# A mixture-of-experts bias that travels with the expert's weights, and a residual that is stored before the routing

## The chip, the cores and the metric

The kernel runs on one core of a Trainium2 chip, and its time is the device time of one execution in microseconds (us). The core has five engines that each work off their own list of instructions in order: TensorE (PE; its weight loads are shown as PEld), VectorE (DVE), ScalarE (ACT), GpSimd (POOL) and SyncE (SP, which here only issues transfers). Transfers between the device's memory and the on-chip memory (SBUF) are done by 16 DMA engines. Results of TensorE land in a second on-chip memory, PSUM, and are fetched from there by DVE or ACT.

## The reference, cut to what matters

Two layers work on 2 x 56 x 56 tokens of 256 numbers. Layer 0 is a neighbourhood attention. Layer 1 has a gated linear attention with a residual, and then the part that the change is in, a mixture of eight experts of which each token uses two:

```python
logits = xf @ gate_w + gate_b
probs = softmax(logits)
top2_vals, top2_idx = top_k(probs, 2)
cw = zeros((N, 8)).at[rows, top2_idx].add(top2_vals)
for w1, b1, w2, b2, we in experts:            # we = cw's column of this expert
    acc += we[:, None] * (gelu(xf @ w1 + b1) @ w2 + b2)
out = x + acc                                 # the layer adds its residual x
```

The second bias b2 (256 numbers for each expert) therefore comes to a token as `cw[token] @ b2`, or, which is the same sum, as `we * b2` beside each of its two experts' results.

## The kernel before, in words

Layer 0 takes about the first 480 us and isn't touched. Layer 1 (`layer_1(False)`, the usual branch) goes over the tokens in 14 steps of 448 (`NST`, `BLK`; four tiles of 112 tokens). For each step, `before_pairs(s)` loads x (`x_acc`, line 730), normalizes it and projects it to q, k and v; `attention(s)` computes the attention, adds its output to x (line 982) and calls `route(s, x)`. `route` normalizes x into `xs`, computes the gate, ranks the eight experts of every token and works out, for both experts that a token uses, the row in which it stands in that expert's region of a buffer `xs_d` in device memory. Eight indirect transfers on POOL's queue (line 1246) write the normalized tokens there. `listed(s)` then lists which tiles of 256 rows (`SL`) have become full. After that `route` adds the second biases: it transposes the combine weights `cw` (line 1260), copies them to SBUF on ACT (line 1262), multiplies them with all eight biases on TensorE (line 1265, `p_b` in the profile), adds the product to x on DVE (line 1266), and stores x to `out` in two transfers on POOL's queue (line 1269).

The experts' tiles are worked off by the generator `experts()`, 56 tiles in all. `fetch(k)` loads a tile's tokens `xg` (line 1372) and the weights `wj` of its expert (line 1376) on SP's queue, two tiles ahead. `gather` transposes the tokens (lines 1386 and 1390), `hidden` computes the first matrix product and the gelu (lines 1400 and 1407), and `results` the second product (line 1431). Before that product `results` makes the tile's row numbers (`rows_e`, line 1415) and combine weights (`own_e` and `cws`, line 1419) on DVE. Each half tile `ye` of 128 rows is scaled out of PSUM by DVE (line 1439), and an indirect transfer on POOL's queue adds it to its rows of `out` (line 1440).

The function `together` interleaves these generators: while attention(s) runs, it advances before_pairs(s+1) and the expert tiles that earlier steps have filled (none in steps 0 to 2, then three or four a step). Two more tiles follow the last step, then the padding of the last rows, and 18 more tiles. This gives a priority to each instruction; the order that stands on each engine is fixed when the kernel is built, and is not always that of the code. Semaphores keep whatever depends on each other in order. Two transfers that both write `out` (or `xs_d`) count as dependent, so each waits for the one before it to have landed.

Buffers: the pool p3 has three buffers (`x_acc`, `xs`, `xg`, `wj`), p6 has six (`ye`, `rows_e`), p2 has two (`cws`), and six PSUM buffers (`mm`) are shared by all the products of a step and a tile.

Of the kernel before, what the change touches and what calls it, by code (L numbers as in the profile page):

```python
# [14 lines left out]
F32 = mybir.dt.float32  # L15
I32 = mybir.dt.int32
U32 = mybir.dt.uint32
AF = mybir.ActivationFunctionType
ALU = mybir.AluOpType
# [4 lines left out]
P = 128  # L24
NB = 2
IMG = 56
L = IMG * IMG
C = 256
NG = 2
# [11 lines left out]
TT = 112  # L41
# [7 lines left out]
NF = FF // P  # L49
# [105 lines left out]
def hybrid_kernel(ctx: ExitStack, tc: tile.TileContext, t: dict, out: bass.AP):  # L155
# [11 lines left out]
    def load(pool, name, shape, src, eng=None, dt=F32):  # L167
        dst = pool.tile(shape, dt, name=name)
        (eng or nc.sync).dma_start(out=dst, in_=src)
        return dst  # L170
# [32 lines left out]
    wgb = load(const, "wgb", [NB * NH, 1], t["L1_attn_wg_b"].unsqueeze(0).to_broadcast([NB * NH, 1]))  # L203
    gw = load(const, "gw", [P, NG, NE], t["L1_ffn_gate_w"].rearrange("(k p) e -> p k e", p=P))
    gb = load(const, "gb", [TT, NE], t["L1_ffn_gate_b"].unsqueeze(0).to_broadcast([TT, NE]))
    b2 = load(const, "b2", [NE, C], t["L1_ffn_b2"])
    before = load(const, "before", [TT, TT], t["before"])
    cand = load(const, "cand", [P, 8 * NE + NX + NE], t["cand"])
    c_row, c_exp, c_num, c_num1 = (
# [429 lines left out]
    def layer_1(general):  # L639
        with (  # L640
# [503 lines left out]

            def route(s, x):


                nonlocal n_prev, c_prev, at_prev
                xs = p3.tile([TT, NTI, ROW], F32, tag="xs", name="xs")
                nc.gpsimd.memset(xs[:, :, CWC + NE :], 0.0)  # L1150
                xT = yield from norm_T(x, "xT_f", p1, xs)
# [103 lines left out]
                listed(s)  # L1255
                yield

                pc = ps_m.tile([NE, NTI, TT], F32, tag="mm", name="p_cw")
                for i in range(NTI):
                    nc.tensor.transpose(pc[:, i, :], cw[:, i, :], ident[:TT, :TT])  # L1260
                cwT = p1.tile([NE, NTI, TT], F32, tag="cwT", name="cwT")
                nc.scalar.copy(cwT, pc)
                for i in range(NTI):
                    ps = ps_m.tile([TT, C], F32, tag="mm", name="p_b2")
                    nc.tensor.matmul(ps, lhsT=cwT[:, i, :], rhs=b2, start=True, stop=True)
                    nc.vector.tensor_tensor(x[:, i, :], ps, x[:, i, :], ALU.add)
                    yield
                for b in range(NB):
                    nc.gpsimd.dma_start(
                        out=out[b * L + s * BT : b * L + (s + 1) * BT].rearrange(  # L1270
                            "(i p) e -> p i e", p=TT
                        ),
                        in_=x[:, b * 2 : (b + 1) * 2, :],
                    )

            def listed(s):


# [74 lines left out]
            def fetch(j):  # L1353

                ent, k = listed_at.pop(j)
                known = "the lists hold rows of the regions and experts alone"
                row = nc.values_load(
                    ent[0:1, 0, k : k + 1],
                    engines=[mybir.EngineType.SP],
                    min_val=0,  # L1360
                    max_val=NE * RG,
                    skip_runtime_bounds_check_because=known,
                )
                exp = nc.values_load(
                    ent[0:1, 1, k : k + 1],
                    engines=[mybir.EngineType.SP],
                    min_val=0,
                    max_val=NE - 1,
                    skip_runtime_bounds_check_because=known,
                )  # L1370
                xg = p3.tile([P, SL // P, ROW], F32, tag="xg", name="xg")
                nc.sync.dma_start(
                    out=xg, in_=xs_d[bass.ds(row, SL), :].rearrange("(u p) c -> p u c", p=P)
                )
                wj = p3.tile([P, NG * FF + NF * C + NF], F32, tag="wj", name="wj")
                nc.sync.dma_start(
                    out=wj, in_=t["we"][bass.ds(exp, 1)].rearrange("o p c -> (o p) c")
                )
                return xg, wj
# [12 lines left out]

            def hidden(xT, wj):
                w1 = wj[:, : NG * FF].rearrange("p (k f) -> p k f", k=NG)
                b1 = wj[:, NG * FF + NF * C :]
                hT = p2.tile([P, NF, SL], F32, tag="hT", name="hT")
                for f in range(NF):
                    ph = ps_h.tile([P, SL], F32, tag="mm", name="p_h")
                    for k in range(NG):
                        nc.tensor.matmul(  # L1400
                            ph,
                            lhsT=w1[:, k, f * P : (f + 1) * P],
                            rhs=xT[:, k, :],
                            start=k == 0,
                            stop=k == NG - 1,
                        )
                    nc.scalar.activation(hT[:, f, :], ph, AF.Gelu, bias=b1[:, f : f + 1])  # L1407
                    yield
                return hT

            def results(j, hT, xg, wj):
                w2 = wj[:, NG * FF : NG * FF + NF * C].rearrange("p (k o) -> p k o", k=NF)

                rows = p6.tile([P, SL // P], I32, tag="rows_e", name="rows_e")
                nc.vector.tensor_copy(rows, xg[:, :, TOK : TOK + 1].rearrange("p u o -> p (u o)"))  # L1415
                cws = p2.tile([P, SL // P], F32, tag="cws", name="cws")
                own = p2.tile([P, NE], F32, tag="own_e", name="own_e")
                for u in range(SL // P):
                    nc.vector.scalar_tensor_tensor(
                        own,  # L1420
                        c_e,
                        l_exp[:, j : j + 1],
                        xg[:, u, CWC : CWC + NE],
                        ALU.is_equal,
                        ALU.mult,
                        accum_out=cws[:, u : u + 1],
                    )
                for u in range(SL // P):
                    py = ps_h.tile([P, C], F32, tag="mm", name="p_y")
                    for f in range(NF):  # L1430
                        nc.tensor.matmul(  # L1431
                            py,
                            lhsT=hT[:, f, u * P : (u + 1) * P],
                            rhs=w2[:, f, :],
                            start=f == 0,
                            stop=f == NF - 1,
                        )
                    y = p6.tile([P, C], F32, tag="ye", name="ye")
                    nc.vector.tensor_scalar_mul(y, py, cws[:, u : u + 1])  # L1439
                    nc.gpsimd.indirect_dma_start(  # L1440
                        out=out[:, :],
                        out_offset=bass.IndirectOffsetOnAxis(
                            ap=rows[:, u : u + 1].bitcast(U32), axis=0
                        ),
                        in_=y,
                        in_offset=None,
                        compute_op=ALU.add,
                    )
                    yield
# [142 lines left out]
```

## Time and profile before

The time is 1860.25 us, the median of three runs (1853.78 to 1864.68). The profiled execution spans 1865.8 us.

| engine | busy us | share of the span |
|---|---|---|
| PE (matmul) | 1504.1 | 81% |
| PEld (weight load) | 1075.6 | 58% |
| DVE | 936.4 | 50% |
| ACT | 626.3 | 34% |
| POOL | 448.5 | 24% |

| stretch of the span, us | what runs there |
|---|---|
| 0 to 480 | layer 0 |
| 480 to 700 | steps 0 to 2 of layer 1, without expert tiles |
| 700 to 1625 | steps 3 to 13, with 36 expert tiles |
| 1625 to 1866 | the last 20 tiles |

How to read it: a line of a group gives the line of the code, the engine, the operation, the tensor written and the tensors read, the number of instructions, their summed busy time, the mean duration of one, the idle time of the engine just before them, and what ended most of that idle time. A line of the timeline gives start, duration, engine and line, and in brackets the idle time before it. In a list of waits, "A <- B: 10.0, 3, 5.0" says that A waited for B three times, 10.0 us in total and 5.0 us at most. A busy share is a mean over stages with different limits, so a stage is read by the wait that ends last in it.

### The profile page before, as it was taken

What the parts mean: (1) busy time and instruction counts of PE and PEld (TensorE: products, weight loads), DVE (VectorE), ACT (ScalarE), POOL (GpSimd) and SP (SyncE); (2) the same over time, 40 slices, a digit from 0 to 9 for tenths busy, and PEclk for the clock granted to TensorE, in tenths of its full rate; (3) what the DMA queues carried; (4) which work ended last, traced back from release to release, by engine and by line L of the source; (5) the groups of instructions that cost most, each with busy time, mean ns of one, the idle gap of its engine ahead of it and who ended that gap; (6) DMA issues with size and microseconds to landing.
All of it is one profiled execution on the core that took longest, in us unless ns stands there. A gap on an engine that the chain in (4) does not pass through costs nothing. (4 is left out here: it accounts for less than half of the span.)

```text
span 1865.8 us, 28574 instructions
## 1 busy us (share of the span) xinstructions
PE 1504.1 (81%) x10840; PEld 1075.6 (58%) x10840; DVE 936.4 (50%) x2787; ACT 626.3 (34%) x1125; POOL 448.5 (24%) x496
## 2 busy tenths in 40 slices
PE   0899999999487778898798879888887888778781
PEld 0466776789254445565465556556565656666670
DVE  3455566654466775655637373746465464411110
ACT  0233433432333233443325333433344241322220
POOL 2123333332101101213131322213131313322232
PEclk9989999975688779899899989898899899989885
DMA  7345554452101103234242414232333324276542
GB/s 227 119 147 168 161 152 145 150 164 85 41 1 41 31 11 127 47 107 109 61 115 63 116 45 126 62 92 71 106 75 98 105 61 109 65 238 170 137 106 27
DMA packets 110786, 190.35 MB, mean 102 GB/s; under 512 B 17674, under 2 KB 92290, under 8 KB 103460
## 3 DMA queue, kind: packets, MB, share of 16 engines
q1 hardware_dynamic: 74612, 128.27, 21.7%
q0 software_dynamic: 32560, 54.55, 13.2%
q10 hardware_dynamic: 3456, 5.51, 0.9%
q8 instruction: 89, 1.46, 0.3%
q14 instruction: 69, 0.57, 0.1%
HBM read 131.52 MB, written 56.73 MB: 101 GB/s over the span
## 5 line engine op out<-in xcount | busy, mean ns | idle before, releaser
L1440 POOL DMA_INDIRECT out<-ye,rows_e x112 | 175.3, 1565 | 635.7 <-DVE ye L1439 206.8
L1400 PE MATMUL p_h<-xT_g,wj 128*128 128x256 f32 x896 | 242.1, 411 | 14.0 <-DVE ye L1439 9.6
L1431 PE MATMUL p_y<-wj,hT 128*128 128x256 f32 x896 | 230.8, 409 | 1.1 <-DVE ye L1439 1.1
L1407 ACT ACTIVATE hT<-p_h,wj 128x256 f32<-128x256 f32 x224 | 105.7, 474 | 351.2 <-PE p_h L1400 317.2
L1400 PEld LDWEIGHTS p_h<-xT_g,wj 128*128 128x128 f32 x896 | 175.8, 204 | 52.6 <-issue 18.2
L1431 PEld LDWEIGHTS p_y<-wj,hT 128*128 128x128 f32 x896 | 178.0, 206 | 38.4 <-issue 9.5
L1246 POOL DMA_INDIRECT xs_d<-xs,rowi x112 | 107.6, 961 | 321.6 <-DMA xs_d<-xs,rowi 129.5
L503 ACT ACTIVATE ex<-ex 98x1024 f32<-98x1024 f32 x98 | 103.8, 1060 | 228.0 <-DVE ex L497 219.2
L1415 DVE CAST rows_e<-xg 128x2 int32<-128x2 f32 x56 | 9.5, 169 | 301.2 <-DMA xg<-xs_d 202.6
L497 DVE TENSOR_TENSOR ex<-sc,bias 98x1024 f32<-98x1024 f32 x98 | 119.7, 1221 | 66.9 <-PE sc L488 65.3
L512 PE MATMUL po<-vw,ex 98*64 98x33 f32 x3136 | 129.2, 240 | 5.8 <-DMA vw<-v_d 5.8
L512 PEld LDWEIGHTS po<-vw,ex 98*64 98x64 f32 x3136 | 117.2, 157 | 23.7 <-DMA vw<-v_d 7.1
L488 PE MATMUL sc<-qb,kc 64*98 64x128 f32 x1568 | 130.0, 311 | 0.0
L488 PEld LDWEIGHTS sc<-qb,kc 64*98 64x98 f32 x1568 | 106.0, 187 | 40.5 <-issue 28.6
L916 PE MATMUL sc<-qh,v 128*112 128x448 f32 x224 | 112.3, 598 | 0.0
L924 DVE TENSOR_TENSOR qv<-sc,upto 112x448 f32<-112x448 f32 x112 | 69.2, 622 | 72.1 <-PE sc L916 70.7
L1439 DVE TENSOR_SCALAR ye<-p_y,cws 128x256 f32<-128x256 f32 x112 | 52.6, 478 | 80.8 <-PE p_y L1431 57.3
L1211 PE MATMUL p_n<-taken,every 112*128 112x32 f32 x28 | 8.2, 383 | 89.9 <-DVE taken L1206 89.9
L315 POOL TENSOR_TENSOR xo<-xo,xq 128x256 f32<-128x256 f32 x49 | 35.6, 727 | 181.4 <-DVE xo L309 173.3
L1386 PE MATMUL pt_g<-ident,xg 128*128 128x128 f32 x224 | 39.4, 304 | 41.1 <-DVE ye L1439 26.2
L954 PE MATMUL po<-qv,kt 112*32 112x112 f32 x896 | 45.7, 277 | 30.9 <-DVE qv L924 30.9
L888 ACT COPY qh<-q 32x448 f32<-32x448 f32 x112 | 63.0, 562 | 2.2
(234 smaller groups left out, 2543.3 us busy)
## 6 DMA issues: line engine op xcount, KB each, us to landing
wj<-in_we SPq DMA_DIRECT2D x56, 1026.0 KB
vw<-v_d SPq DMA_DIRECT2D x196, 101.1 KB
xg<-xs_d SPq DMA_DIRECT2D x56, 272.0 KB
v_d<-values POOLq DMA_DIRECT2D x28, 231.0 KB, 3.7
xq<-in_x SPq DMA_DIRECT2D x98, 64.0 KB
q_d<-evq POOLq DMA_DIRECT2D x28, 224.0 KB, 3.0
qb<-q_d SPq DMA_DIRECT2D x56, 112.0 KB
x_d<-xo POOLq DMA_DIRECT2D x98, 64.0 KB, 3.1
```

The source lines that it names most:

```text
L488: nc.tensor.matmul(sc[:KN, p, b, k], lhsT=keys(i, j, k, b, rows, g), rhs=qb[rows, g, :, b, j * QN : (j + 1) * QN], start=True, stop=True,)
L497: nc.vector.tensor_tensor(ex[:KN], sc[:KN].rearrange("n p b k h q -> n p b (k h q)"), tables[kind][:KN, g].unsqueeze(2).to_broadcast(wide) ...
L503: nc.scalar.activation(ex[:KN], ex[:KN], AF.Exp)
L512: nc.tensor.matmul(po[b * QN : (b + 1) * QN, hh, :], lhsT=ex[:KN, p, b, k, h, :], rhs=vw[:KN, b, k, hh * (HD + 1) : (hh + 1) * (HD + 1)], ...
L888: nc.scalar.copy(qh[hp, h, :], qg[hp])
L916: nc.tensor.matmul(sc, lhsT=vg[:, i * TT : (i + 1) * TT], rhs=qh[:, :, i * TT : (i + 1) * TT], start=True, stop=True,)
L924: nc.vector.tensor_tensor(qv, sc, upto.unsqueeze(1).to_broadcast([TT, 4, TT]), ALU.mult)
L1246: nc.gpsimd.indirect_dma_start(out=xs_d[:, :], out_offset=bass.IndirectOffsetOnAxis(ap=rowi[:, c, i : i + 1].bitcast(U32), axis=0), in_=xs ...
L1400: nc.tensor.matmul(ph, lhsT=w1[:, k, f * P : (f + 1) * P], rhs=xT[:, k, :], start=k == 0, stop=k == NG - 1,)
L1407: nc.scalar.activation(hT[:, f, :], ph, AF.Gelu, bias=b1[:, f : f + 1])
L1431: nc.tensor.matmul(py, lhsT=hT[:, f, u * P : (u + 1) * P], rhs=w2[:, f, :], start=f == 0, stop=f == NF - 1,)
L1440: nc.gpsimd.indirect_dma_start(out=out[:, :], out_offset=bass.IndirectOffsetOnAxis(ap=rows[:, u : u + 1].bitcast(U32), axis=0), in_=y, in_ ...
```

## The change

The second bias no longer passes through TensorE. The weights' record of an expert in device memory gets 256 more columns that hold b2, repeated for all 128 partitions, so b2 arrives with `wj`. For each half tile ACT writes b2 times the combine weight into the result buffer `ye` before the second product, and DVE adds the scaled product to it in one instruction. The routing then has nothing more to add to x, so it stores x at its start.

```diff
-    b2 = load(const, "b2", [NE, C], t["L1_ffn_b2"])
...
             def route(s, x):
                 nonlocal n_prev, c_prev, at_prev
+                for b in range(NB):
+                    nc.gpsimd.dma_start(
+                        out=out[b * L + s * BT : b * L + (s + 1) * BT].rearrange(
+                            "(i p) e -> p i e", p=TT
+                        ),
+                        in_=x[:, b * 2 : (b + 1) * 2, :],
+                    )
...
                 listed(s)
                 yield
-                pc = ps_m.tile([NE, NTI, TT], F32, tag="mm", name="p_cw")
-                for i in range(NTI):
-                    nc.tensor.transpose(pc[:, i, :], cw[:, i, :], ident[:TT, :TT])
-                cwT = p1.tile([NE, NTI, TT], F32, tag="cwT", name="cwT")
-                nc.scalar.copy(cwT, pc)
-                for i in range(NTI):
-                    ps = ps_m.tile([TT, C], F32, tag="mm", name="p_b2")
-                    nc.tensor.matmul(ps, lhsT=cwT[:, i, :], rhs=b2, start=True, stop=True)
-                    nc.vector.tensor_tensor(x[:, i, :], ps, x[:, i, :], ALU.add)
-                    yield
-                for b in range(NB):
-                    nc.gpsimd.dma_start(
-                        out=out[b * L + s * BT : b * L + (s + 1) * BT].rearrange(
-                            "(i p) e -> p i e", p=TT
-                        ),
-                        in_=x[:, b * 2 : (b + 1) * 2, :],
-                    )
...
-                wj = p3.tile([P, NG * FF + NF * C + NF], F32, tag="wj", name="wj")
+                wj = p3.tile([P, NG * FF + NF * C + NF + C], F32, tag="wj", name="wj")
...
+                b2 = wj[:, NG * FF + NF * C + NF :]
+                ys = []
                 for u in range(SL // P):
+                    y = p6.tile([P, C], F32, tag="ye", name="ye")
+                    nc.scalar.activation(y, b2, AF.Copy, scale=cws[:, u : u + 1])
+                    ys.append(y)
+                for u, y in enumerate(ys):
                     py = ps_h.tile([P, C], F32, tag="mm", name="p_y")
...
-                    y = p6.tile([P, C], F32, tag="ye", name="ye")
-                    nc.vector.tensor_scalar_mul(y, py, cws[:, u : u + 1])
+                    nc.vector.scalar_tensor_tensor(
+                        y, py, cws[:, u : u + 1], y, ALU.mult, ALU.add
+                    )
...
                 a["L1_ffn_b1"].reshape(NE, NF, P).transpose(0, 2, 1),
+                np.repeat(a["L1_ffn_b2"][:, None, :], P, axis=1),
```

More of the change, by code (lines that the diff above doesn't have):

```diff
@@ L1394, in hidden @@
                 w1 = wj[:, : NG * FF].rearrange("p (k f) -> p k f", k=NG)
-                b1 = wj[:, NG * FF + NF * C :]
+                b1 = wj[:, NG * FF + NF * C : NG * FF + NF * C + NF]
                 hT = p2.tile([P, NF, SL], F32, tag="hT", name="hT")
@@ L1572 @@
         "L1_ffn_gate_b",
-        "L1_ffn_b2",
     ):
```

## The prediction

> **What bounds the kernel now.** I read the windows of equal length first (TensorE busy 52 to 63 of each 67 us from 637 to 1575), then the chain of waits from the end, POOL's and TensorE's timelines, and the waits of each engine between 770 and 1610 us. Layer 1 has two regimes.
>
> The last regime runs from about 1645 us to the end. The chain of waits consists there of nothing but the scatter-adds into `out` (start, length, what):
>
> ```profile
> 1809.06 3.75 DMA out<-ye,rows_e
> 1812.85 0.05 issue
> 1812.90 0.49 DVE ye L1439
> 1813.40 0.16 issue
> 1813.56 3.71 DMA out<-ye,rows_e
> ```
>
> Each waits for the one before to land: 1813.56 - 1809.06 = 4.50 us when nothing else moves. POOL's timeline has 38 of them from 1645.68 to 1854.83. TensorE does a tile in about 7.4 us there (16 matmuls in 3.62 us, twice, and four transposes), a pair of scatter-adds takes 9.0 us or more, so TensorE, DVE and ACT all wait for buffers. Only the number of scatter-adds and what slows one can change this stretch.
>
> The steps 4 to 13 take about 86.5 us each. TensorE works nearly without gaps, but each step has a gap of 1 to 5 us that DVE causes:
>
> ```profile
> 1404.43 0.47 PE L949 MATMUL po<-q,zc 128*128 128x112 f32 x2
> 1408.60 0.60 PE L954 MATMUL po<-qv,kt 112*32 112x112 f32 x8 [3.70 <-DVE qv L924]
> ```
>
> ```profile
> PE po L954 <- DVE qv L924: 30.9, 13, 5.5
> ...
> DVE rows_e L1415 <- DMA xg<-xs_d: 155.2, 34, 10.9
> ```
>
> DVE stands at `rows_e`, for tokens that it needs only half a step later, with the attention's `qv` queued behind it. The tokens come late because POOL writes `xs_d` in eight transfers that each wait for the last:
>
> ```profile
> 1381.05 0.96 POOL L1246 DMA_INDIRECT xs_d<-xs,rowi  x1 [0.31 <-issue]
> 1383.24 0.73 POOL L1269 DMA_DIRECT2D out<-x_acc  x1 [1.23 <-DMA out<-ye,rows_e]
> 1384.28 0.98 POOL L1246 DMA_INDIRECT xs_d<-xs,rowi  x1 [0.30 <-issue]
> 1385.26 0.71 POOL L1269 DMA_DIRECT2D out<-x_acc  x1
> 1387.21 0.97 POOL L1246 DMA_INDIRECT xs_d<-xs,rowi  x1 [1.24 <-DMA xs_d<-xs,rowi]
> 1390.11 0.94 POOL L1246 DMA_INDIRECT xs_d<-xs,rowi  x1 [1.93 <-DMA xs_d<-xs,rowi]
> ```
>
> Undisturbed they follow at 2.88 us (1387.21 to 1390.11). The residual's two stores and two to three scatter-adds sit among them, and SP's load of the next `x_acc`, released by the store, runs beside them. So the gate in each of these steps is: row numbers ready, eight writes, `xg` of two or three tiles, `rows_e`, `qv`.
>
> Steps 0 to 2 have no tiles. There TensorE stands between 692.65 and 697.75 in the removed work, with the next step behind it:
>
> ```profile
> 692.65 0.93 PE L1260 MATMUL p_cw<-ident,xs 112*8 112x112 f32 x4
> 694.20 3.75 PE L1265 MATMUL p_b<-b,cwT 8*112 8x256 f32 x8 [0.61 <-ACT cwT L1262]
> 697.75 0.32 PE L876 MATMUL p_gt<-ident,gl 16*112 16x16 f32 x2
> ```
>
> [...] 2.6 us from issue to landing for `xs_d`, 2.9 us for the residual, 3.9 us (median) for an accumulating scatter. [...] the copies of lines 1390 and 1262 stand between gelus with no table load of theirs, while a load takes 1.28 us. [...]
>
> **The change part by part.** Prices first, from the groups kept apart by shape (count | busy us, mean ns | idle us before and what ended it):
>
> ```profile
> L1265 PE MATMUL p_b<-b,cwT 8*112 8x256 f32 x112 | 35.2, 436 | 8.9 <-ACT cwT L1262 5.8 <-DVE l_row L1342 2.4 <-DVE c L1296 0.7
> ...
> L760 DVE SCALAR_TENSOR_TENSOR pd<-p_qkv,bq,k 128x448 f32<-128x448 f32 x28 | 19.1, 684 | 44.0 <-ACT q L758 44.0
> ...
> L417 DVE TENSOR_SCALAR evq<-pq,bq 128x448 f32<-128x448 f32 x28 | 19.1, 682 | 16.6 <-PE pq L406 15.2 <-DMA x_d<-xo 0.9
> ```
>
> *Removed from the routing, 14 times:* four transposes and eight matmul passes, 0.55 + 2.2 = 2.8 us of TensorE at full clock (1455.71 to 1460.80 with other work between) and up to 5.1 us where the clock is down and ACT's copy is waited for (692.65 to 697.75); four DVE adds of line 1266, 4 x 0.417 = 1.67 us; one ACT copy, 0.52 us. What is it worth? At the end of step 0 DVE is the limit (TensorE waits 7.46 us for `gl`): 1.7 us. At the ends of steps 1 and 2 TensorE would be 5.1 us earlier, but DVE is busy without a gap until the next step's `kt`; its 1.67 us go, and with TensorE ahead so do DVE's first waits for it (0.43, 0.61, 1.01): 3.5 us each. Sum for steps 0 to 2: 8.7 us. From step 3 on, these 2.8 to 3.2 us lie between the row numbers and the gate, and TensorE would only reach the gate sooner and wait longer. I take nothing for them there.
>
> *Moved:* the two stores leave the row of eight writes. In POOL's timeline I took, for each of the ten routings from 765 to 1570 us, the gaps that hold a store or follow the `x_acc` load, and subtracted what a clean 2.88 us would give: 0.4 to 2.9 us, 1.8 on average. That is the gain of the gate per step. In its new place the store waits for the last add of line 982 and for the previous scatter-add. Behind it on POOL stand the memset of `xs` and the tile's scatter-adds. POOL idles there (20.2 us before 1429.91, 15.5 us before 1454.61), so a delay of some 1.5 us of one scatter-add costs nothing.
>
> *Added to the loads:* 128 partitions x 1 KB = 128 KB on 1026 KB. From 1398.51 to 1411.1 us three `xg` and two `wj` (2868 KB) came in, 228 KB per us, so 128 KB are 0.56 us. The second `xg` stands behind one `wj` and the third behind two: 0.56 or 1.1 us later, 0.75 on average. Gate per step: -1.8 + 0.75 = -1.05, times ten = -10.5 us. The last routing's row of writes loses its stores too: -1.5 us.
>
> In the last regime 18 scatter-adds took 99.8 us (1704.10 to 1803.87), 11.09 us a tile against 8.96 alone. So loading 1298 KB a tile costs 2.13 us, and 128 KB more cost 0.21 us; times 18 tiles: +4 us. If the tokens' share weighed nothing it would be 0.27 us, 5 us.
>
> *Added on ACT:* two scaled copies of 128x256 for each tile. The trace has 562 ns for a copy of 448 columns from SBUF (line 888). [...] the gelu's 474 ns is the upper end. I take 420 ns: 112 x 0.42 = 47 us on an engine that is 34% busy, hidden in TensorE's time. New is what the copy waits for: `own_e` of DVE, the landing of `wj`, and a `ye` buffer, that is, the scatter-add of three tiles before. Behind it on ACT stand the tile's gelus, the next tile's token copy and the attention's copies; TensorE waits for all of those. Before the last regime the buffer is free in time: `own_e` is done after that scatter-add has landed for each tile up to 40. The weights are not always there. For the first tile after a gate `own_e` ends at 1402.9 and `wj`, issued at 1399.5, lands near 1406. That is inside DVE's own stall (to 1407.85), so I take 0, up to 4 us a step. In the last regime the copy waits for the scatter-add too, but two tiles (four scatter-adds, 18 us) are still queued behind it, more than TensorE's 7.4 us.
>
> *On DVE:* the new instruction reads PSUM and one more tensor. 684 against 682 ns above for the same shapes: no cost.
>
> Sum: -8.7 - 10.5 - 1.5 + 4 = -16.7 us, 1843.5 us.
>
> **The rivals.** *TensorE is the limit in every step* (for: no gap but the short ones; against: each step has one): the full 3 us come out of all 14 steps, 42 - 4 = 38 us, 1822 us. *The gate doesn't move* (for: the longer weights and some other interleaving eat the 1.8 us; scatter-adds remain among the writes): -8.7 + 4, 1855 us. *ACT becomes the new place of the stall* (for: in-order copies that need weights and a free buffer, put early in its list as `rows_e` was on DVE; against: DVE already stands still then): 11 steps x up to 4 us and some in the last stretch, +30 us against -16.7, about 1873 us, slower than before.
>
> **How the numbers follow.** The first case 0.42, TensorE 0.13, the unmoved gate 0.25, ACT 0.20. The range reaches from 1818 (below the TensorE case) to 1872, near the ACT case. Faster by over 9.3 us holds for most of the first case, the second, and a little of the third: 0.60. Same 0.24, slower 0.16.
>
> **What would show it.** Right: `po <- qv` still 2 to 6 us a step, the first of the eight writes to the last about 2 us shorter, steps of some 85.5 us, the same 38 scatter-adds from the last stretch's start at about 11.3 us a pair. Wrong: ACT's scaled copy high in the list of waits with TensorE behind it, steps over 87 us, or steps of 83 us and no gate.

## The result and the profile after

The kernel after takes 1808.28 us, the median of four runs (1801.35 to 1821.23), against 1862.47 us before (1853.78 to 1870.11): a ratio of 0.9719 with a 95% interval of 0.9648 to 0.9789. I had forecast 1843.5 us and a range from 1818 to 1872. The change gives three times what I forecast.

The time of a run goes with the clock that TensorE is granted in it, as a mean over the run: a straight line through the 219 runs of all kernels of this study, with one level for each kernel and one common slope, has 15 us for 0.01 of clock and leaves 5 us of scatter. In the profiled runs the stretch up to layer 1's first `p_gt` (layer 0 and the first projections of layer 1), which the experiments change by no more than a small constant, took from 486.7 us (e1, granted clock 0.948 in it) to 523.6 us (e13, 0.864). So the times of the experiments are given at a common clock of 0.885, from that line, with 95% intervals. There the kernel before takes 1862.8 us and the kernel after 1810.2 us, 52.6 +- 5.3 us less, which is what the plain medians say too. Some runs of a kernel are over 1.5% slower than its fastest, at a lower clock; a line through the other 131 runs moves no difference by more than 5.3 us (e3: 29.8 in place of 24.5 us less than before). The words "steps 3 to 12" stand for the time from the `p_n` of step 3 to that of step 13 in the profiled run; they are not put at a common clock.

Where did the time go? First the windows of steps 3 to 12 in before, then the same in after: start and end, length, busy time of PE, PEld, DVE, ACT and POOL with the number of instructions, PE's clock, the DMA share and GB/s.

```profile
760.46:1605.33 844.87, 717.20 (x3802) 500.41 (x3803) 460.46 (x1593) 314.11 (x543) 202.45 (x178) 0.91 0.33 88
```

```profile
758.60:1553.96 795.36, 672.20 (x3682) 484.32 (x3683) 447.08 (x1547) 340.58 (x610) 202.71 (x177) 0.91 0.35 98
```

The ten steps lose 49.5 us at the same clock. TensorE is busy 45.0 us less, and it stands still nearly as long as before (127.7 and 123.2 us). The removed rows `p_cw` and `p_b` were 29.7 us of TensorE there, and `p_sum`, with as many instructions as before, goes from 35.0 to 15.4 us; some other rows are longer. The section on the turns comes back to `p_sum`. The other stretches hardly matter: the first `p_gt` to `p_n` of step 3 (steps 0 to 2) goes from 245.1 to 236.0 us, `p_n` of step 13 to the first of the last 38 scatter-adds from 40.35 to 40.25 us, and these 38 from 209.15 to 214.14 us. The stretch up to the first `p_gt` took 7.3 us more in the profiled run of after; its clock was nearly the same (0.873 and 0.875), so the reason is open.

The chain of waits still ends in scatter-adds, each behind the landing of the last:

```profile
1793.43 0.71 issue
1794.14 3.67 DMA out<-ye,rows_e
...
1803.14 0.71 issue
1803.85 3.75 DMA out<-ye,rows_e
1808.36 1.54 POOL out L1434
```

TensorE's and DVE's longest waits in steps 3 to 12 of after (total us, times, longest) are the same as before, in the same order. First TensorE's longest of before, then those of after:

```profile
PE p_n L1211 <- DVE taken L1206: 63.4, 10, 8.4
```

```profile
PE p_n L1216 <- DVE taken L1211: 71.4, 10, 8.0
PE po L953 <- DVE qv L923: 16.8, 9, 3.0
...
PE p_qkv L749 <- DVE ye L1431: 8.2, 4, 3.1
```

```profile
DVE rows_e L1402 <- DMA xg<-xs_d: 139.5, 31, 9.3
```

So the gate is still there: DVE stands at `rows_e` for 139.5 us (before 155.2), and TensorE waits at `po` for the `qv` behind it, 16.8 us where it was 30.9. The first of the two waits, for `taken` at `p_n`, is the largest of TensorE's waits in both kernels (63.4 us before). I had not counted on it as anything that could change.

POOL's row of eight writes in the routing that answers to the one shown of before:

```profile
1337.45 0.96 POOL L1251 DMA_INDIRECT xs_d<-xs,rowi  x1 [0.31 <-issue]
1339.95 1.57 POOL L1434 DMA_INDIRECT out<-ye,rows_e  x1 [1.54 <-DMA out<-ye,rows_e]
1341.82 0.96 POOL L1251 DMA_INDIRECT xs_d<-xs,rowi  x1 [0.31 <-issue]
1346.51 0.96 POOL L1251 DMA_INDIRECT xs_d<-xs,rowi  x1 [3.72 <-DMA xs_d<-xs,rowi]
1349.38 0.93 POOL L1251 DMA_INDIRECT xs_d<-xs,rowi  x1 [1.92 <-DMA xs_d<-xs,rowi]
```

The residual's stores are gone from it, but the long gap is not: 1341.82 to 1346.51 is 4.69 us with a scatter-add just ahead of the first of the two writes, where a clean pair takes 2.87 us. A scatter-add there doesn't always do that: of the 11 writes that directly follow one in the ten steps of after, six let the next go after 2.83 to 3.10 us and five after 3.81 to 5.37. Over the ten steps the row goes from 23.9 to 23.35 us, 0.56 us a step.

The new instructions, by groups with shapes kept apart (count | busy us, mean ns | idle before and its releasers):

```profile
L1431 DVE SCALAR_TENSOR_TENSOR ye<-p_y,cws,ye 128x256 f32<-128x256 f32 x112 | 53.8, 480 | 206.6 <-PE p_y L1424 189.8 <-issue 16.5
L1419 ACT ACTIVATE ye<-wj,cws 128x256 f32<-128x256 f32 x112 | 53.2, 504 | 233.4 <-DMA wj<-in_we 92.9 <-DMA out<-ye,rows_e 70.4 <-DVE own_e L1406 70.0
L1148 POOL DMA_DIRECT2D out<-x_acc x28 | 20.3, 725 | 149.5 <-DVE x_acc L981 88.4 <-DVE lmv L696 30.5 <-DMA out<-ye,rows_e 13.2
```

DVE's instruction costs what the old one did (480 against 478 ns), ACT's 504 ns. ACT does stand for the weights, up to 10.0 us at a time, but among TensorE's waits in steps 3 to 12 there is only one for ACT, 4.7 us for `xT_f`, and that isn't the copy.

### The profile page after: what moved, and what is told of

Read it like the earlier page. It is cut to its first block, busy times and chain, and to the rows that moved or that the text cites. A ratio compares the mean times of both kernels' runs of the same rounds, so it can differ in the third digit from the quotient of the medians.

```text
span 1819.4 us, 28420 instructions
## 1 busy us (share of the span) xinstructions
PE 1445.9 (79%) x10672; PEld 1056.6 (58%) x10672; DVE 920.4 (51%) x2731; ACT 667.0 (37%) x1233; POOL 450.9 (25%) x496
## 5 line engine op out<-in xcount | busy, mean ns | idle before, releaser
L1424 PE MATMUL p_y<-wj,hT 128*128 128x256 f32 x896 | 249.1, 432 | 46.5 <-ACT hT L1394 46.5
L1424 PEld LDWEIGHTS p_y<-wj,hT 128*128 128x128 f32 x896 | 190.4, 220 | 87.8 <-ACT hT L1394 52.3
L1387 PE MATMUL p_h<-xT_g,wj 128*128 128x256 f32 x896 | 229.4, 394 | 4.6 <-DMA wj<-in_we 4.6
L1387 PEld LDWEIGHTS p_h<-xT_g,wj 128*128 128x128 f32 x896 | 170.6, 197 | 43.0 <-issue 21.2
L1431 DVE SCALAR_TENSOR_TENSOR ye<-p_y,cws,ye 128x256 f32<-128x256 f32 x112 | 53.8, 480 | 206.6 <-PE p_y L1424 189.8
L1394 ACT ACTIVATE hT<-p_h,wj 128x256 f32<-128x256 f32 x224 | 100.3, 469 | 139.9 <-PE p_h L1387 138.6
L1419 ACT ACTIVATE ye<-wj,cws 128x256 f32<-128x256 f32 x112 | 53.2, 504 | 233.4 <-DMA wj<-in_we 92.9
L915 PE MATMUL sc<-qh,v 128*112 128x448 f32 x224 | 105.2, 572 | 7.1 <-DVE kt L893 7.1
L436 ACT ACTIVATE kc<-pk,bk 128x112 f32<-128x112 f32 x196 | 50.4, 369 | 39.5 <-PE pk L405 39.5
L405 PE MATMUL pq<-xs,L_wqT 128*128 128x448 f32 x112 | 54.6, 617 | 12.7 <-DVE top L439 12.7
```

Of the source, the lines that this page charges most:

```text
L405: nc.tensor.matmul(ps, lhsT=w[:, k, g * P : (g + 1) * P], rhs=xs[:, b, k, :], start=k == 0, stop=k == NG - 1,)
L915: nc.tensor.matmul(sc, lhsT=vg[:, i * TT : (i + 1) * TT], rhs=qh[:, :, i * TT : (i + 1) * TT], start=True, stop=True,)
L1387: nc.tensor.matmul(ph, lhsT=w1[:, k, f * P : (f + 1) * P], rhs=xT[:, k, :], start=k == 0, stop=k == NG - 1,)
L1424: nc.tensor.matmul(py, lhsT=hT[:, f, u * P : (u + 1) * P], rhs=w2[:, f, :], start=f == 0, stop=f == NF - 1,)
```

## The experiments

All times are at a clock of 0.885, with the difference from before; the last columns are of the profiled run. "turns" are the four `yield` of the bias loop, at which `together` gets to advance the other generators.

| run | what it is | us | minus before | steps 3 to 12 | waits for qv |
|---|---|---|---|---|---|
| before | | 1862.8 | | 844.9 | 30.9 |
| e4 | before, experts of after | 1856.1 | -6.7 +- 2.6 | 830.5 | 20.4 |
| e3 | before without the turns | 1838.3 | -24.5 +- 5.3 | 824.7 | 26.6 |
| e9 | e3 without the adds | 1852.7 | -10.1 +- 5.3 | 832.6 | 35.1 |
| e10 | e3, TensorE's part twice | 1851.4 | -11.4 +- 5.3 | 831.9 | 2.5 |
| e2 | before without block, with turns | 1821.0 | -41.8 +- 2.7 | 805.0 | 40.6 |
| e1 | before without block or turns | 1810.3 | -52.5 +- 5.3 | 805.2 | 11.3 |
| e6 | e1 with four adds | 1802.8 | -60.0 +- 5.3 | 796.0 | 20.9 |
| e13 | e1 with eight products | 1840.9 | -21.9 +- 3.2 | 831.3 | 36.2 |
| e17 | e13 in one PSUM buffer | 1838.9 | -23.9 +- 2.6 | 831.1 | 36.1 |
| e18 | e13, 16 columns each | 1820.7 | -42.1 +- 5.3 | 804.4 | 18.6 |
| e14 | e1 with transposes and ACT's copy | 1822.1 | -40.7 +- 5.3 | 803.5 | 23.5 |
| e5 | e1 with the stores first | 1814.8 | -48.0 +- 5.3 | 807.9 | 27.8 |
| after | | 1810.2 | -52.6 +- 5.3 | 795.4 | 16.8 |
| e11 | after with four empty turns | 1815.0 | -47.8 +- 5.3 | 791.9 | 29.5 |
| e16 | before, rows_e late | 1830.9 | -31.9 +- 5.6 | 800.5 | 4.4 |
| e8 | after, rows_e late | 1798.8 | -64.0 +- 5.3 | 778.3 | 3.5 |
| e15 | after, PAUSE 12 | 1782.4 | -80.5 +- 5.4 | 755.8 | 4.3 |
| e12 | after, rows_e late and PAUSE 12 | 1774.2 | -88.6 +- 5.3 | 744.3 | 4.1 |

Two cautions go with the table. The runs stand in groups on different chips, each with its own runs of before, whose levels at the common clock lie between 1860.1 and 1865.7 us. Measured against the before of its own group, e13 is 26 us above e1 (from the table 31), e17 23 (29), e14 7 (12), e18 5 (10), e10 8 above e3 (13), and e9 9 above e3 (14). And the granted clock in steps 3 to 12 was 0.90 to 0.92 in most profiled runs, but 0.93 in e4, e8, e15 and e16 and 0.95 in e12, so in these five a part of the shorter steps is clock.

The first theory of the result was that TensorE's removed work comes out in full (theory one) and that the four turns, by which the build orders the instructions, matter by themselves (theory two); the rival was my own prediction, the gate and the moved stores.

### Which part of the change gains: e1, e5, e4

e1_no_block takes the block out of the routing and leaves the stores at its end:

```diff
-                pc = ps_m.tile([NE, NTI, TT], F32, tag="mm", name="p_cw")
...
-                    nc.tensor.matmul(ps, lhsT=cwT[:, i, :], rhs=b2, start=True, stop=True)
-                    nc.vector.tensor_tensor(x[:, i, :], ps, x[:, i, :], ALU.add)
-                    yield
```

> The routing loses the whole block of the second bias (transposes, copy, eight matmul passes, four adds and the four turns that its loop hands to the interleaving); the two stores stay at its end and the experts are as before. The bias is left out of the result. Before: 1862 us, steps 3 to 12 844.9 us. If the block is what the change gained by (turns and TensorE's work together): steps 3 to 12 about 800 us, first row write 4.2 us after p_n, time 1862 - 9 - 45 = about 1808 us. If the moved stores and the gate are the gain, as my prediction had it: steps 3 to 12 about 843 us, time about 1853 us.

e5_stores_first differs from e1 by the place of the stores:

```diff
                 nonlocal n_prev, c_prev, at_prev
+                for b in range(NB):
+                    nc.gpsimd.dma_start(
...
                 listed(s)
                 yield
-                for b in range(NB):
-                    nc.gpsimd.dma_start(
```

> The routing of after (no bias block, both residual stores at its start) with the experts of before; the bias is left out of the result. It differs from e1_no_block by the place of the stores alone. Gate theory of my prediction (the row of eight writes sets the step and loses 1.8 us): steps 3 to 12 go from 805 to about 787 us, the time from about 1810 to about 1790 us at the same clock. TensorE theory: the writes may get shorter but the step doesn't; steps 3 to 12 within 5 us of 805, time within 6 us of e1_no_block.

e4_experts_half is the other half of the change; to make room its block multiplies by another weight and copies half of `cwT`, as the expectation says:

```diff
-                wj = p3.tile([P, NG * FF + NF * C + NF], F32, tag="wj", name="wj")
+                wj = p3.tile([P, NG * FF + NF * C + NF + C], F32, tag="wj", name="wj")
...
+                    nc.scalar.activation(y, b2, AF.Copy, scale=cws[:, u : u + 1])
...
-                    nc.vector.tensor_scalar_mul(y, py, cws[:, u : u + 1])
+                    nc.vector.scalar_tensor_tensor(
+                        y, py, cws[:, u : u + 1], y, ALU.mult, ALU.add
+                    )
```

> The routing of before with its block and its stores at the end, and the experts of after: weights of 1154 KB with their biases, ACT's scaled copy, DVE's instruction with three operands. To make room, the block multiplies by rows of another weight in place of b2 and copies half the columns of cwT, so the output has another term in place of the bias. If the expert half only costs: the last chain of 38 scatter-adds 209 to 214 us, ACT's copies hidden, time 1862 + 4 to + 8, about 1868 us. If the experts' new order is where the gain came from: below 1850 us. If ACT stalls TensorE: steps 3 to 12 over 860 us, about 1880 us.

Measured: the block with its turns is worth 52.5 us, all that the change brings. No gain by moving the stores is seen (e5 less e1 is +4.5 +- 7.5 us; the row of writes shrinks from 23.66 to 23.07 us a step and the steps don't). No cost of the experts' half is seen either; if anything it gains a few us (e4 6.7 +- 2.6, after less e5 4.6 +- 7.5). So the gate theory's term for the stores falls, and the question is what in the block was dear.

### The turns: e2, e3, e11

e2_no_block_turns keeps the loop and empties it; e3_block_no_turns keeps all the work and drops the `yield`; e11_after_turns puts four empty turns into after.

In e2:

```diff
-                for i in range(NTI):
-                    ps = ps_m.tile([TT, C], F32, tag="mm", name="p_b2")
...
+                for _ in range(NTI):
                     yield
```

In e3:

```diff
                     nc.vector.tensor_tensor(x[:, i, :], ps, x[:, i, :], ALU.add)
-                    yield
```

In e11:

```diff
                 listed(s)
                 yield
+                for _ in range(NTI):
+                    yield
```

> As e1_no_block, but the loop of four turns is kept with nothing in it; the bias is left out of the result. Theory of the turns (four turns fewer put the next step's reciprocals ahead of p_n): first row write stays 6.9 us after p_n on average, steps 3 to 12 about 824 us, time about 1831 us. Theory of TensorE's work alone: steps 3 to 12 about 800 us and time about 1808 us, as without the turns. Gate theory of my prediction: about 1853 us.

> The kernel before with its four turns taken out of the bias loop and nothing else; all work stays. Theory of the turns: first row write 4.2 us after p_n in every step instead of 5.2 and 8.1 in turn, steps 3 to 12 shorter by 20 to 25 us, time about 1840 us. Theory of TensorE's work alone, and the gate theory: within 4 us of 1862 us.

> The kernel after with four empty turns at the end of its routing, where the bias loop had its four; no work is added. Theory of the turns: first row write 5 to 8 us after p_n in place of 4.2 and p_sum slower in every other step, steps 3 to 12 longer by 10 to 20 us, time 1820 to 1830 us at a clock of 0.885. If turns count only while TensorE has the block's work to do (e1 and e2 had equal steps 3 to 12): within 5 us of 795 us and 1810 us.

Without removing any work, e3 gains 24.5 us. Its trace shows two differences. In before, every other step has the next step's `p_sum` between transposes that wait for DVE's `xs`. TensorE's timeline of before, in the step ahead of the one shown above:

```profile
1345.23 0.32 PE L718 MATMUL pt_x<-ident,xs 112*128 112x112 f32 x1 [2.61 <-DVE xs L707]
1345.48 0.62 PE L784 MATMUL p_sum<-pd,ind 128*16 128x224 f32 x2
1346.03 0.45 PE L718 MATMUL pt_x<-ident,xs 112*128 112x112 f32 x1
1346.41 0.94 PE L784 MATMUL p_sum<-pd,ind 128*16 128x224 f32 x4
...
1348.90 2.44 PE L784 MATMUL p_sum<-pd,ind 128*16 128x224 f32 x22
```

The same work in e3:

```profile
1326.96 1.71 PE L784 MATMUL p_sum<-pd,ind 128*16 128x224 f32 x32
1328.60 0.47 PE L949 MATMUL po<-q,zc 128*128 128x112 f32 x2
1330.47 0.32 PE L718 MATMUL pt_x<-ident,xs 112*128 112x112 f32 x1 [1.40 <-DVE xs L707]
```

Behind the wait a `p_sum` takes 0.11 us and more, ahead of it 0.05 us; over steps 3 to 12 that makes 35.0 against 15.4 us of TensorE, as much as the 20.2 us that these steps lose. The trace also has the reason for the doubled time. TensorE's granted clock (the third number from the end) was half behind that wait in before, and full again from 1352.66:

```profile
1346.00:1352.60 6.60, 6.60 (x40) 2.88 (x40) 3.11 (x7) 0.82 (x2) 0.00 (x0) 0.50 0.00 0
1352.70:1362.80 10.10, 7.87 (x48) 6.80 (x46) 7.13 (x22) 9.86 (x14) 1.55 (x1) 1.00 0.27 80
```

The other difference is on DVE: the reciprocals and scans of the next step, which in before stand between `p_n` and the row numbers, come ahead of `p_n`, so the first write follows `p_n` after 4.2 us in place of 8.1 and 5.2 in turn. That moves the gate ahead by 25 us in ten steps, and 4.7 us of it come back behind the gate. But theory two holds only beside the block. Once the block is gone the turns are worth 10.7 +- 6 us (e2 less e1) with equal steps 3 to 12, and in after they are worth 4.8 +- 7.5 us. Yet e2 and e11, which have the turns, show both differences too: `p_sum` takes 29.2 and 32.4 us in their steps 3 to 12 (15.4 in e1 and after), and the first writes come as late as in before, and their steps are no longer than those of e1 and after. So neither difference is shown to be the cause of e3's 24.5 us; why the turns cost beside the block stays open.

### What in the block costs: e9, e10, e6, e7

e9_products_only is e3 without its adds; e10_products_twice is e3 with each transpose and product done twice; e6_adds_only is e1 with four adds of zeros.

In e9:

```diff
-                    nc.vector.tensor_tensor(x[:, i, :], ps, x[:, i, :], ALU.add)
```

In e10:

```diff
                     nc.tensor.transpose(pc[:, i, :], cw[:, i, :], ident[:TT, :TT])
+                    nc.tensor.transpose(pc[:, i, :], cw[:, i, :], ident[:TT, :TT])
...
                     nc.tensor.matmul(ps, lhsT=cwT[:, i, :], rhs=b2, start=True, stop=True)
+                    nc.tensor.matmul(ps, lhsT=cwT[:, i, :], rhs=b2, start=True, stop=True)
```

In e6:

```diff
+                for i in range(NTI):
+                    nc.vector.tensor_tensor(x[:, i, :], zb, x[:, i, :], ALU.add)
```

> e3_block_no_turns (1838 us at a clock of 0.885, steps 3 to 12 824.7 us) without the four DVE adds of the bias, and nothing else changed (e7_products_only had lost the attention's residual adds as well): transposes, copy and products stay, unread, and the bias is left out. TensorE theory: steps 3 to 12 within 6 us of 825 us, with TensorE busy about 700 us, and about 1836 us. DVE theory: the block's 1.67 us of DVE a step are what the change gained by: about 805 us and about 1812 us.

> e3_block_no_turns with each of the four transposes and four products of the bias done twice into the same place: 2.8 to 3.0 us of TensorE a step more, same result, same turns, same adds. TensorE theory: steps 3 to 12 longer by 25 to 32 us, about 852 us; time about 1838 + 14 x 2.9 = 1878 us at the same clock. Gate theory (TensorE waits for the tokens in any case): steps 3 to 12 within 6 us of 825 us, time below 1848 us.

> e1_no_block with four DVE adds of 112x256 put back, of a tile of zeros in SBUF in place of the product, without turns and without any of the block's work on TensorE and ACT; the bias is left out. TensorE theory: steps 3 to 12 about 805 us as in e1_no_block, time about 1810 us at the same clock. If the 1.67 us of DVE a step were what counts: about 822 us as in e3_block_no_turns, time about 1834 us.

> e3_block_no_turns without its four adds: transposes, copy and eight matmul passes stay, nothing reads the product, no turns; the bias is left out. TensorE theory: steps 3 to 12 about 825 us as in e3_block_no_turns (TensorE busy about 700 us of them), time about 1838 us at the same clock. DVE theory: about 805 us and about 1813 us.

e7_products_only left out more than its text says, the four adds of the attention's output to x as well (line 982), so it tells nothing of the products; it took 1792.8 us, and e9 takes its place. That it was 60 us faster than e9, with the products still in it, hints that these adds or what waits for them are dear, but without them the gate also ranks other numbers, and no run follows it up.

DVE's adds in the bias block are not seen as a cost. Taking them away made e9 14 +- 7.5 us slower than e3, and putting them into e1 made e6 7.5 +- 7.5 us faster. No operation explains either sign. In both, the build lays out the lists of all engines anew; I take that for the cause, which isn't shown, and a part is noise. Differences of that size are given to no cause below. Theory one got a blow from e10: doing TensorE's part a second time, 36.5 us more in its rows `p_cw` and `p_b`, cost 13 +- 7.5 us. TensorE's waits in steps 3 to 12 say where it went, first e3, then e10:

```profile
PE p_n L1211 <- DVE taken L1206: 71.4, 10, 7.9
PE po L954 <- DVE qv L924: 26.6, 11, 4.0
```

```profile
PE p_n L1211 <- DVE taken L1206: 71.1, 10, 7.9
...
PE po L954 <- DVE qv L924: 2.5, 1, 2.5
```

24 us of the wait at the gate were filled, as my prediction has it for work ahead of the gate. So why didn't the first 3 us a step fill it?

### Products, copy, or PSUM buffers: e13, e14, e17, e18

All four are e1 with a piece of the block put back, unread. e13_products_const has the eight passes from a constant, e14_transposes_only the transposes and the copy, e17_one_buffer the passes of e13 in one PSUM buffer, e18_short_products those of e13 with 16 columns:

In e13:

```diff
+                for i in range(NTI):
+                    ps = ps_m.tile([TT, C], F32, tag="mm", name="p_b2")
+                    nc.tensor.matmul(ps, lhsT=ident[:NE, :TT], rhs=b2, start=True, stop=True)
```

In e17, against e13:

```diff
-                for i in range(NTI):
-                    ps = ps_m.tile([TT, C], F32, tag="mm", name="p_b2")
+                ps = ps_m.tile([TT, C], F32, tag="mm", name="p_b2")
+                for i in range(NTI):
```

In e18, against e13:

```diff
-                    nc.tensor.matmul(ps, lhsT=ident[:NE, :TT], rhs=b2, start=True, stop=True)
+                    nc.tensor.matmul(ps[:, :16], lhsT=ident[:NE, :TT], rhs=b2[:, :16], start=True, stop=True)
```

> e1_no_block with only the eight matmul passes of the bias put back, from a constant in place of the transposed weights, unread: 2.2 us of TensorE and four PSUM buffers a step, no transposes, no copy on ACT, no wait for it, no adds, no turns; the bias is left out. If TensorE's time or the PSUM buffers made the block's price: steps 3 to 12 about 822 to 830 us, time about 1830 us at a clock of 0.885. If the chain with ACT made it: about 805 us and about 1812 us, as in e1_no_block.

> e1_no_block with only the four transposes and ACT's copy put back, their result unread: 0.55 us of TensorE and 0.52 us of ACT a step, no products, no adds, no turns; the bias is left out. If TensorE's time made the price: within 6 us of e1_no_block (805 us for steps 3 to 12, 1810 us in all). If a place in the lists of ACT and PSUM made it: about 820 us and about 1830 us.

> e13_products_const with all eight passes of a step written into one PSUM buffer in place of four: the same 2.2 us of TensorE a step, three buffers fewer taken from the shared six; the bias is left out. If TensorE's time made the price: steps 3 to 12 about 830 us, time about 1840 us at a clock of 0.885. If the buffers made it: about 805 to 810 us, time about 1815 us.

> e13_products_const with products of 16 columns in place of 256: four PSUM buffers a step as before, and about 0.5 us of TensorE a step in place of 2.2; the bias is left out. If the buffers made the price: steps 3 to 12 about 830 us, time about 1840 us at a clock of 0.885. If TensorE's time made it: about 808 us, time about 1815 us.

The products carry the price: e13 is 30.6 +- 6 us above e1 (26 against the before of its own group), and its row of the products has 31.4 us of TensorE in all 14 steps. In total that is about one for one. The buffers don't matter (e17 as e13), the columns do: e18, with 14.8 us of products (1.06 us a step, where I had expected 0.5), is 20.2 +- 6 us below e13. What is left above e1, 10.4 +- 7.5 us in e18 and 11.8 +- 7.5 us in e14 with the transposes and the copy, is hardly clear of the noise, and their steps 3 to 12 are no longer than e1's (at a granted clock of 0.92 and 0.91 in them against 0.90). TensorE's waits of e13 and of e1 show the surprise:

```profile
PE p_n L1211 <- DVE taken L1206: 71.1, 10, 7.9
PE po L954 <- DVE qv L924: 36.2, 14, 6.0
...
PE sc L916 <- DVE kt L894: 11.3, 6, 2.8
```

```profile
PE p_n L1211 <- DVE taken L1206: 71.1, 10, 7.9
...
PE po L954 <- DVE qv L924: 11.3, 6, 4.2
PE p_qkv L750 <- DVE ye L1429: 10.7, 4, 4.0
```

With 19.8 us of products less to do in ten steps TensorE doesn't wait longer behind DVE's stall, it waits less: 47.5 us for `qv` and `kt` in e13, 34.4 us for `qv`, `kt` and `ye` in e1. And the 71 us at `p_n` stay to the tenth of a us. So the ten steps lose 26.1 us, more than the products themselves. I read a step as a loop on TensorE's list, from one `p_n` to the next with a constant wait of 7 us in it, in which what is taken out of the list comes out of the step, unless the wait at the gate grows in its place. In e1 and after it did not grow on removal; in e2, the block out and the turns kept, it grew from 30.9 to 40.6 us, a third of the 29.7 us removed; and it shrank when e10 added. I can't say why these differ. The lists do (in e10 246 passes of `p_h` stand between `p_n` and the second `rows_e`, 12 us behind the last write, in the ten steps together, in e3 and e1 284), but no run tests that as a cause, and it stays open.

### Was the gate a limit, and is there a better kernel: e16, e8, e15, e12

In e16_before_rows_late and e8_rows_late, `rows_e` is made from `cws`, which has two buffers, so it can't be placed early:

```diff
-                nc.vector.tensor_copy(rows, xg[:, :, TOK : TOK + 1].rearrange("p u o -> p (u o)"))
...
+                nc.vector.scalar_tensor_tensor(
+                    rows, cws, 0.0, xg[:, :, TOK : TOK + 1].rearrange("p u o -> p (u o)"), ALU.mult, ALU.add
+                )
```

e15_after_pause has six more turns between `taken` and `p_n`, and e12_rows_late_pause both edits:

```diff
-PAUSE = 6
+PAUSE = 12
```

> The kernel before, with its block and its turns, with rows_e made from cws so that DVE doesn't stand at it for the second and third tile. If the gate that my prediction worked with sets the steps of the kernel before: the 31 us of TensorE's waits for qv go, steps 3 to 12 about 815 to 825 us, time about 1835 us at a clock of 0.885. If another wait takes its place: within 6 us of 845 us and 1861 us.

> The kernel after, with rows_e made from the tile's cws (times zero) and its token column, so that DVE can't reach it before the combine weights and no longer stands in front of the attention's qv for tiles that it needs later. Gate theory: DVE's waits at rows_e for xg (about 28 us of every two steps) go, TensorE's waits for qv and kt go with them, up to 4 us a step: steps 3 to 12 about 765 us, time about 1775 us. TensorE theory: the idle time turns up at another wait and only a part of it is saved: steps 3 to 12 between 780 and 795 us, time 1793 to 1808 us. If the scatter-adds, whose row numbers come later now, are delayed: over 1810 us.

> The kernel after with PAUSE 12 in place of 6 and rows_e where it was. If the wait at p_n (71 us in steps 3 to 12) is a matter of order alone: steps 3 to 12 about 760 us, time about 1780 us. If the stall at rows_e holds the step whatever stands before p_n: about 795 us and about 1810 us, and e12_rows_late_pause gains only with both.

> e8_rows_late (1799 us at a clock of 0.885, steps 3 to 12 778 us, of which TensorE waits 73.5 us for taken at p_n) with PAUSE 12 in place of 6: six more turns between taken and p_n, so more of TensorE's other work stands in front of p_n in its list. If that wait is only a matter of order: it falls to below 40 us, steps 3 to 12 about 750 us, time about 1770 us. If the row numbers then come later and the gate with them: the wait moves to own_e and qv, and the time is 1795 to 1810 us.

The gate was a limit of the kernel before: without it e16 is 31.9 us faster, and of TensorE's 30.9 us at `qv` 4.4 are left. Its steps 3 to 12 lose 44.4 us: TensorE stands still 29.2 us less, and it is busy 15.2 us less with the same instructions (702.0 against 717.2 us), as its granted clock in them rose from 0.91 to 0.93 (717.2 x 0.91 / 0.93 is 701.8). So the clock is in part an outcome of the edit, and the common clock of the table takes that part of the gain away: the recorded ratio of e16 to before, not put at a common clock, is 0.9758 (0.9639 to 0.9877), some 45 us. In after the gate is worth 11.4 +- 7.5 us (e8). DVE's waits of e16 in steps 3 to 12 show that only the first tile's tokens are still waited for:

```profile
DVE ye L1441 <- PE p_y L1433: 65.4, 48, 4.2
DVE qv L924 <- PE sc L916: 62.7, 57, 2.3
DVE own_e L1418 <- DMA xg<-xs_d: 54.2, 10, 9.1
```

The greater gain is at `p_n`. In e12 the wait for `taken` is nearly gone, and no other takes its place in full:

```profile
PE pt_x L717 <- DVE xs L706: 24.3, 10, 7.1
PE pt_g L1373 <- DMA xg<-xs_d: 20.5, 6, 5.1
PE p_out L974 <- DVE q L964: 16.6, 7, 4.0
PE p_n L1216 <- DVE taken L1211: 7.9, 5, 2.7
```

The first write comes 12.0 us after `p_n` of the same step on average, but `p_n` itself no longer holds up what stands behind it, and the ten steps take 744.3 us, at a granted clock of 0.95 in them. e12 took 1769.05 us (median of four runs, 1737.26 to 1783.74), a ratio to before of 0.9369 (0.9274 to 0.9465); e15 with the pause alone 1766.23 us (1753.18 to 1772.66), 0.9579 (0.9507 to 0.9652), at a higher clock. At a common clock e12 is 36 us faster than after. Both beat the kernels before and after; between the two the 8 us are too few to choose by.

## Why the prediction was wrong, point by point

**The step that failed** is the one on the removed work: "From step 3 on, these 2.8 to 3.2 us lie between the row numbers and the gate, and TensorE would only reach the gate sooner and wait longer. I take nothing for them there." Measured, nearly all of the gain is there: steps 3 to 12 lose 49.5 of the 52.6 us. Work put in ahead of the gate did fill the wait (e10). The work taken out didn't lengthen it: the waits for `qv` went from 30.9 to 16.8 us in after and from 36.2 to 11.3 us between e13 and e1, and for the 31.4 us of the products 23 to 31 us came out (e13 and e17 against e1). Only in e2 did they grow, by 9.7 us. Why the wait doesn't take up the time, as it should if the gate alone set the step, stays open. I saw TensorE busy 52 to 63 of every 67 us and "a gap of 1 to 5 us" in each step, and took that gap for the limit. It isn't the only one: in each of the ten steps TensorE also stands 4.4 to 8.4 us at `p_n`, 63.4 us in all, twice its waits for `qv`. The rival that TensorE limits every step, 1822 us, to which I gave 0.13, was the nearer one, though 14 us short.

**What no step of mine had** is the order. I counted instructions and looked where each stands in the trace of before, as if the rest of the lists would stay. The four `yield` that go with the block change where the next step's instructions stand on DVE and TensorE, and beside the block they alone are worth 24.5 +- 5.3 us (e3). The parts don't add up: with the turns kept the block's work is worth 41.8 us, without them 28.0 us; together 52.5 us.

**The moved stores**, 1.8 us a step and 1.5 us in the last routing: the mechanism is there and the size is not. The row of eight writes lost 0.56 us a step and 0.86 us in the last routing, and no gain in time is seen from it (e5 against e1; the stretch from the last routing to the last scatter-adds lost 0.1 us). I had put every gap that holds a store down to the store; after shows long gaps in rows that hold scatter-adds alone (the 4.69 us above).

**The longer weights**, 0.75 us a step at the gate: from the last write to the second `rows_e` the ten steps take 117.9 us before and 118.2 us after, so 0.03 us a step. As for the last stretch, +4 us: the 38 scatter-adds took 5.0 us more, but that agreement is accidental. e4, with the longer weights, has 205.2 us there and e1, with the short ones, 213.3 us. What sets that stretch within these 10 us is open.

**Steps 0 to 2**, -8.7 us: 9.1 us measured, from 245.1 to 236.0. The reasons are not confirmed, since e1 has 242.6 us there at a clock of 0.81 and e5 235.7 us at 0.83.

**ACT**: 504 ns for the copy, above the 420 ns that I took and above my upper end, the gelu's 474 ns. The 420 ns were an estimate of mine: no copy of 128x256 in the trace of before shows them. No table load stands at the copy's line in after, though ACT's loads in the whole kernel go from 74 to 84, at 1.28 us each. The copy is hidden all the same; the rival in which ACT becomes the new stall was right about ACT (it waits 81 us for `wj` in steps 3 to 12) and wrong about TensorE, which doesn't wait for it. **DVE**: no cost, as forecast (480 against 478 ns). **The gate**: a real limit in before, as I read it, 31.9 us by e16; only the change did little to it.

## What to carry to other kernels

When a trace shows one engine nearly full with a short gap in each period, price removed work of that engine both ways, in full and at nothing, and don't let the gap decide: here the gap shrank with the work in most variants. And count what a wait costs beyond its own length: behind it TensorE may run at half clock for a while (in before at 0.50 from 0.6 to 7.4 us behind the end of a wait of 2.61 us), so look at the granted clock of the stretch before naming a slow row's cause. In a kernel whose order is laid out by a build, removing a yield is a change of its own; make the variant that drops the work and keeps the yields, and the one that keeps the work and drops the yields. And look for the longest wait that stays nearly constant through the variants (here 6 to 7 us a step at `p_n`): in after it was worth another 28 us, more than half of what the change brought, for one number in the source.

## What the runs showed of the hardware that I had not expected

Behind most gaps of TensorE stands a stretch at half clock, so that a gap can cost more than its own length. The traces' record of the granted clock has two values only, 0.5 and 1.0. In steps 3 to 12 of before TensorE has 23 waits of 2 us and more (the shortest 2.1 us); for each of them a stretch at half clock begins before the wait ends or at most 1.8 us behind its end. In after that holds for 15 of 17 such waits; for one of 2.5 us the stretch begins 2.6 us behind its end, and behind one of 2.7 us there is none. One stretch in before and three in after stand behind no such wait. The ten steps of before hold 148.6 us at half clock, in 112.1 of which TensorE was busy; in e12, with the wait at `p_n` nearly gone, it is 81.7 and 74.5 us. A `p_sum` in a row of them takes 0.11 us at half clock (22 in 2.44 us in before) and 0.05 us at full (32 in 1.71 us in after).

An indirect write into `xs_d` right behind a scatter-add into `out`, with which it shares no bytes, can let the next write go late (five of 11 times in the ten steps of after, 3.81 to 5.37 us in place of 2.87), but it need not; three gaps behind a write that follows a write are long too (3.41 to 3.73 us), and what decides isn't shown. And ACT takes 504 ns for a copy of 128x256 scaled by a column, hardly less than the 562 ns for the unscaled copy of 32x448 in the trace of before.
